# A mixture of experts on one core: a DRAIN one unit sooner, first products on ones, and four groups of transposes elsewhere in the head

## The chip, the cores and the metric

The kernel runs on one core of a Trainium2 chip. The metric is the device time of the kernel in microseconds; the runs of the kernel before gave 457.3, 457.4 and 457.6, and the median, 457.4 us, is what a changed kernel is compared with.

## The reference, cut to what matters

4096 tokens of 256 values go through a gate, which chooses two of eight experts for each. An expert is three layers (256 to 512, 512 to 512, 512 to 256). The reference computes all experts for all tokens and weights them; the kernel computes only those chosen.

```python
var = jnp.mean(x * x, axis=-1, keepdims=True)
xn = rms_w * (x * jax.lax.rsqrt(var + EPS))
gate = xn @ wg_W + wg_b + (genre_embed @ gg_W + gg_b)
gate_w = jax.nn.softmax(gate, axis=-1)
topk_w, topk_i = jax.lax.top_k(gate_w, TOP_K)
cw = jnp.sum(jax.nn.one_hot(topk_i, E, dtype=x.dtype) * topk_w[..., None], axis=-2)
h1 = jax.nn.relu(jnp.einsum('bsh,ehm->bsem', x, W1) + b1)
h2 = jax.nn.relu(jnp.einsum('bsem,emn->bsen', h1, W2) + b2)
out_e = jnp.einsum('bsen,enh->bseh', h2, W3) + b3
return x + jnp.einsum('bseh,bse->bsh', out_e, cw)
```

Here x has 64 x 64 tokens, `genre_embed` is one row of 64 values for each group of 64 tokens, and all is float32.

## The kernel before, in words

The order of the instructions on each engine is written out by hand (`tc.manual_schedule`); the framework adds the waits.

**The head.** x lies in SBUF as 32 columns of 128 tokens, loaded in eight groups of four (`load_x`; group j is `xin[j]`). The gate needs x with its 256 values on the partitions, so each group is transposed by TensorE in two halves c = 0, 1. `turn_pe(j, c, bank)` (line 247) writes four 128 x 128 transposes into one PSUM bank, `TB[bank]`, where `TB` is the banks 0, 1, 2, 5, 4. `turn_copy(n, eng, bank)` copies that bank to place n, on VectorE ("V", line 258) or ScalarE ("A", line 260). `turn` is one after the other. `gates` and `gates_2` multiply the copied places by the gate's weights (lines 265 and 278), `upright` and `upright_2` turn the result back (lines 291 and 284).

The first eight columns (part A, groups 0 and 1) are routed at once, so that the first expert units can start: `first_part` normalises, chooses two experts for each token (`choose`, VectorE), counts ranks on TensorE (`ranks`, lines 399 and 400), finds each token's place in its expert's list (`pick`), builds one-hot tables (line 535) and multiplies them out to the list of tokens (line 539). With that list GpSimd gathers the first unit's rows (line 844). While part A is in work, the other groups are transposed in between. `second_part` goes on with part B, of which `some(n)` sums squares of n columns on VectorE; `transpose_x(0)` turns the rows gathered for unit 0, and `layer1(0)` follows (line 1015). `third_part` stands between `layer1(0)` and `layer2(0)` (line 1025).

Ahead of all this, `busy(n)` (line 301) issues n transposes of the 128 x 128 identity into a bank that nobody reads yet. The identity is made by GpSimd; `ones` is a 128 x 128 tile that VectorE fills first of all (line 152).

**The units.** Eight units of 128 tokens, one for each expert, come first, then units of four, two or one tiles of 128 places. Line 1124 is the products of layers 1 and 2 in the larger units, lines 1246 and 1214 those of layer 3. The routing of part B (`rest`) runs on VectorE beside the first eight units; its last tables are multiplied in line 604. For each tile, `give` forms weighted rows on VectorE (line 1262) and GpSimd adds them to the output by an indirect DMA (line 1263). A write waits for writes of the unit before to land, since a token's row is read and written back.

**The tail.** The number and sizes of the last units depend on the data; `tc.Switch` chooses one of several programs for them. `steps` runs unit u's layers 1 and 2 with unit u - 1's layer 3 and writes. In the unit after the last (u = last) only the last unit's layer 3 and its writes remain. GpSimd gets one DRAIN in the tail (line 1556); the program's end (line 1638) has others on every engine, and SyncE's waits for the landing of all DMAs.

```python
            if u == last - 1:
                nc.gpsimd.drain()
```

Of the kernel before, what the change touches and what calls it, by code (L numbers as in the profile page):

```python
# [52 lines left out]
def kernel(  # L53
# [17 lines left out]
    nc = tc.nc  # L71
    V = nc.vector
    P = 128
# [12 lines left out]
    GA = NA // TPB  # L86
# [30 lines left out]
    PB = [psum.tile([P, 512], F32, tag=f"pb{k}", name=f"pb{k}") for k in range(8)]  # L117
# [6 lines left out]
    def ring(pool, shape, tag, bufs, b, dt=F32):  # L124

        if tag not in rings:
            rings[tag] = [buf(pool, shape, f"{tag}_{k}", dt) for k in range(bufs)]
        return rings[tag][b % bufs]
# [17 lines left out]
    ident = const.tile([P, P], F32, name="ident")  # L146
# [4 lines left out]
    ones = const.tile([P, P], F32, name="ones")  # L151
# [50 lines left out]
    def load_x(j, n=1):  # L202
        k = j % (NG - GA)
        nc.sync.dma_start(
            big[:, k : k + n], xr[:, j * TPB : (j + n) * TPB, :].rearrange("p (j k) h -> p j k h", j=n)
        )
# [26 lines left out]
    def squares(i, eng):  # L233
        xi = xin[i // TPB][:, i % TPB, :]
        if eng == "A":
            nc.scalar.activation(sqs[eng], xi, AF.Square, accum_out=ss[:, i : i + 1])
        else:
            V.tensor_tensor_reduce(sqs[eng], xi, xi, 1.0, 0.0, ALU.mult, ALU.add, ss[:, i : i + 1])

    def turn(j, c, n, eng, bank):  # L240

        turn_pe(j, c, bank)
        turn_copy(n, eng, bank)

    def turn_pe(j, c, bank):
        for k in range(TPB):
            nc.tensor.transpose(TB[bank][:, ts(k, P)], xin[j][:, k, ts(c, P)], ident)  # L247

    def turned(n):

        if n < 4:
            return hid[1][:, n]
        return bigf[:, 2 * TPB * H + (n - 4) * TPB * P :][:, 0 : TPB * P]

    def turn_copy(n, eng, bank):
        tp, xTc = TB[bank], turned(n)
        if eng == "V":
            V.tensor_copy(xTc, tp)
        else:
            nc.scalar.copy(xTc, tp)  # L260

    def gates(c, bufs):

        for q, n in enumerate(bufs):
            nc.tensor.matmul(
                PB[3][32 * q : 32 * q + 32, :],
                lhsT=wg_sb[:, c, :],
                rhs=turned(n),
                start=c == 0,
                stop=c == HC - 1,  # L270
            )

    def gates_2(bufs, bank):

        for q, ns in enumerate(bufs):
            for c, n in enumerate(ns):
                r = 32 * (2 * c + q)
                nc.tensor.matmul(bank[r : r + 32, :], lhsT=wg_sb[:, c, :], rhs=turned(n), start=True, stop=True)  # L278
# [19 lines left out]
    def busy(n):  # L298

        for _ in range(n):  # L300
            nc.tensor.transpose(PB[3][:, 0:P], ident, ident)

    class Part:

# [146 lines left out]
    def some(n):  # L451
        for _ in range(n):
            squares(left.pop(0), "V")

    def first_part():


        rw2 = gTs[0:HC, 0:P]
        load_x(0)
        nc.scalar.dma_start(wg_in, wg_W.rearrange("(c p) e -> p c e", p=P))  # L460
        load_x(1)
        nc.scalar.dma_start(rw2, rms_w.rearrange("(c p) -> c p", c=HC))
        load_x(2, 2)
        nc.scalar.dma_start(gg_sb[0:G, :], gg_W)
        load_x(4, 2)
        nc.scalar.sqrt(warm, ones[:, 0:E])
        V.memset(wg_sb, 0.0)
        V.memset(condT[G : G + 2, :, :], 1.0)
        V.memset(cw8B, 0.0)
        for k in range(3):  # L470
            V.memset(ring(run, [P, H], "xg", 3, k), 0.0)
        V.memset(cgR, 0.0)
        nc.gpsimd.dma_start(cwdA.rearrange("(p i) e -> p i e", p=P)[:, NA:NI, :], cw8B[:, NA:NI, :])
        busy(7)
        rwp, cps, gps = PB[7][:, P : P + HC], PB[7][0:G, 2 * P : 2 * P + B], PB[7][:, 3 * P : 3 * P + E]
        nc.tensor.transpose(rwp, rw2, ident[:HC, :HC])
        V.tensor_copy(rwT, rwp)
        for c in range(HC):
            V.tensor_scalar(wg_sb[:, c, 0:E], wg_in[:, c, :], rwT[:, c : c + 1], None, ALU.mult)
        for i in (2, 3):  # L480
            squares(i, "A")
        turn(0, 0, 0, "V", 0)
        turn(0, 1, 1, "A", 1)
        squares(0, "V")
        turn(1, 0, 2, "V", 2)
        squares(TPB + 2, "A")
        turn(1, 1, 3, "A", 3)
        squares(TPB + 3, "A")
        nc.tensor.transpose(cps, cond_sb, ident[:B, :B])
        for i in (1, TPB, TPB + 1):  # L490
            squares(i, "V")
        V.tensor_copy(condT[0:G], cps.unsqueeze(2).to_broadcast([G, B, REP]))
        for j in range(NG - GA, NG):
            load_x(j)
        nc.sync.dma_start(vecs[0 : E * MC, :], b1.rearrange("e (c p) -> (e c) p", p=P))
        nc.sync.dma_start(vecs[E * MC : 2 * E * MC, :], b2.rearrange("e (c p) -> (e c) p", p=P))
        load_weights(0, (0, 1))
        gates_2(((0, 1), (2, 3)), PB[3])
        nc.scalar.copy(gTs, PB[3])
        pA.norm(True)  # L500
        turn(GA, 0, 0, "A", 0)
        nc.tensor.matmul(gps, lhsT=condT.rearrange("g b r -> g (b r)"), rhs=gg_sb, start=True, stop=True)
        V.tensor_copy(ggate, gps)
        row_numbers(0)
        chosen = pA.choose(upright_2(PB[4]))
        for q in (1, 2, 3):
            turn(GA + q, 0, q, "A", q)
        turn_pe(GA, 1, 0)
        next(chosen)
        turn_pe(GA + 1, 1, 4)  # L510
        for _ in chosen:
            pass
        pA.ranks()
        V.tensor_tensor(
            mvA.rearrange("p (k i) e -> p k i e", k=TOPK),
            pA.ohe.rearrange("p k e i -> p k i e"),
            toka.unsqueeze(1).unsqueeze(3).to_broadcast([P, TOPK, NA, E]),
            ALU.mult,
        )
        row_numbers(1)  # L520
        pA.exps()
        gates(0, range(4))
        turn_pe(GA + 2, 1, 1)
        turn_copy(0, "A", 0)
        turn_copy(1, "A", 4)
        turn_copy(2, "A", 1)
        V.scalar_tensor_tensor(
            pA.slot, pA.inc[:, 1:].rearrange("p (e i) -> p e i", e=E), -1.0, pA.along(pA.adj), ALU.add, ALU.add
        )
        pA.pick(lo16A.rearrange("p (k i) -> p k i", k=TOPK))  # L530
        tabA = PB[7][:, 0:E]
        GH = GC // 4
        for g0 in range(0, GC, GH):
            hs = slice(g0, g0 + GH)
            V.tensor_tensor(
                ohA[:, :, hs], iotx[:, :, hs], lo16A[:, hs].unsqueeze(1).to_broadcast([P, P, GH]), ALU.is_equal
            )
            for g in range(g0, g0 + GH):
                nc.tensor.matmul(tabA, lhsT=ohA[:, :, g], rhs=mvA[:, g, :], start=(g == 0), stop=(g == GC - 1))
        pA.totals()  # L540
        turn(GA + 3, 1, 3, "A", 2)

        V.tensor_scalar(sa[:, 0:E], tabA, 0.0, float(NT), ALU.is_equal, ALU.mult)
        V.scalar_tensor_tensor(idxA, tabA, float(OFFA), sa[:, 0:E], ALU.add, ALU.add)
        V.tensor_copy(totA1, pA.tot)
# [19 lines left out]
    def second_part():  # L565

        j0 = GA + 4
        vps = PB[6][:, 384 : 384 + 2 * E * MC]
        pA.weights()
        some(1)  # L570
        nc.tensor.transpose(vps, vecs, ident[: 2 * E * MC, : 2 * E * MC])
        V.tensor_copy(vT.rearrange("p l e c -> p (l e c)"), vps)
        some(1)
        turn(j0, 0, 4, "A", 3)
        some(2)
        turn(j0 + 1, 0, 6, "A", 0)
        gates(1, range(4))
        some(2)
        transpose_x(0)
        nc.scalar.copy(gTs, PB[3])  # L580
        turn(j0, 1, 5, "V", 3)
        some(4)

    def third_part():

        turn(GA + 5, 1, 7, "V", 3)
        some(len(left))
        raw = upright()
        nc.scalar.copy(graw[:, NA : NA + 4 * TPB, :].rearrange("p (q k) e -> p q k e", q=4), raw)
        gates_2(((4, 5), (6, 7)), PB[7])  # L590
        nc.scalar.copy(gTs, PB[7])
# [955 lines left out]
    def steps(u0, u1, last):  # L1547
        for u in range(u0, u1):
            if u < last and paired(u):
                step_fast(u, last)  # L1550
            else:
                step(u, last)
                if u < last:
                    layer2(u)
            if u == last - 1:
                nc.gpsimd.drain()

    CUT = E + NQT - 2
# [44 lines left out]
    for k in tc.Switch(arm, len(ARMS), hint="tail"):  # L1603
# [5 lines left out]
        last = E + len(plan)  # L1609
# [33 lines left out]
```

## Time and profile before

| what | us |
|---|---|
| runs, median (lowest to highest) | 457.4 (457.3 to 457.6) |
| the profiled execution's own time | 457.79 |
| its span | 456.0 |
| busy: TensorE's products | 443.9 |
| busy: VectorE | 364.9 |
| busy: GpSimd | 270.8 |
| busy: ScalarE | 240.2 |
| first transpose of the identity | starts at 2.62 |
| first gather (unit 0) | issued at 19.66 |
| layer 1 of unit 0 | starts at 23.57 |
| the DRAIN of line 1556 | 8.925 long, from 439.0 |
| last write | issued at 450.64 |

Times within the profile count from the start of its span. The profiled execution's own time holds 1.8 us more than the span, and lies 0.4 us above the median of the runs, which were taken without a profile. "Busy" counts overlapping instructions of an engine once. A matmul's end in the profile is modelled and later than the start of the next one, so a series is read by its starts.

### The profile page before, as it was taken

How to read it: one execution, taken by the hardware profiler on the slowest of the kernel's cores; microseconds unless marked ns; L12 is line 12 of the kernel's file. 1: busy time of each engine (PE TensorE's matmuls, PEld its weight loads, DVE VectorE, ACT ScalarE, POOL GpSimd, SP SyncE). 2: the span in 40 equal slices, each digit the busy share in tenths (PEclk: the TensorE clock that was granted, in tenths of full speed). 3: DMA queues.
4: the chain of work that ended last, by engine and by line, in shares of the span. 5: the costliest groups of instructions: out<-in, count | busy, mean ns of one | idle time of the engine just before them, and what ended most of it. 6: DMA issues, size and time to landing. Idle time of an engine off the chain costs nothing.

```text
span 456.0 us, 9190 instructions
## 1 busy us (share of the span) xinstructions
PE 443.9 (97%) x2942; PEld 410.0 (90%) x2942; DVE 364.9 (80%) x961; ACT 240.2 (53%) x559; POOL 270.8 (59%) x231
## 2 busy tenths in 40 slices
PE   7899999999999999999999999999999999999993
PEld 5689999968989898989999999999999889999992
DVE  5887897269797979798988988887877887988861
ACT  4746553435646373828365656464464355565551
POOL 4255532867787868677675656578646645664222
PEclk9999999999999999999999999999999999999998
DMA  8699999793766858374655555666656664675322
GB/s 294 251 308 376 378 366 385 283 271 79 188 160 133 180 108 193 76 166 108 131 125 125 117 123 116 130 180 137 144 149 115 156 162 93 163 177 143 70 24 27
DMA packets 75631, 78.76 MB, mean 173 GB/s; under 512 B 34927, under 2 KB 64082, under 8 KB 75188
## 3 DMA queue, kind: packets, MB, share of 16 engines
q1 hardware_dynamic: 48976, 43.29, 30.0%
q0 software_dynamic: 14960, 17.47, 22.6%
q10 hardware_dynamic: 11636, 17.32, 11.9%
q8 instruction: 25, 0.41, 0.4%
q14 instruction: 34, 0.28, 0.2%
HBM read 62.60 MB, written 20.12 MB: 181 GB/s over the span
## 4 chain that ended last, share of the span: by engine, by line
PE 90%; issue 3%; DMA 2%; ACT 1%; POOLq 1%; DVE 0%; POOL 0%; ACTq 0%
PE pb L1124 52%; PE pb L1246 12%; PE pb L1214 11%; PE pb L1025 6%; PE pb L1015 5%; PE pb L247 1%; DMA out_dram<-ys,idxR 1%; PE pb L604 1%; DMA gTs<-in_L_cond_rms_w_dram 1%; PE pb L911 1%; DMA xg<-in_x_dram,idxA 1%; PE pb L278 1%; POOLq L1638 1%; POOL out_dram L1263 0%; PE pb L284 0%
## 5 line engine op out<-in xcount | busy, mean ns | idle before, releaser
L1263 POOL DMA_INDIRECT out_dram<-ys,idxR x59 | 96.7, 1639 | 94.7 <-DVE ys L1262 41.6
L1124 PE MATMUL pb<-hid,big 128*128 128x256 f32 (+7 forms) x456 | 83.4, 326 | 0.0
L1145 ACT ACTIVATE hid<-hid,bb 128x256 f32<-128x256 f32 (+13 forms) x148 | 70.4, 524 | 16.6 <-DVE hid L1142 9.9
L844 POOL DMA_INDIRECT cg<-cwdR,idxR x59 | 67.6, 1145 | 18.0 <-issue 17.4
L1124 PEld LDWEIGHTS pb<-hid,big 128*128 128x128 f32 x456 | 71.4, 191 | 5.1 <-issue 1.0
L1246 PE MATMUL pb<-w3r,hid 128*128 128x256 f32 (+3 forms) x280 | 66.2, 380 | 0.0
L1133 ACT COPY q1s<-pb 128x256 f32<-128x256 f32 (+7 forms) x54 | 25.4, 470 | 59.5 <-PE pb L1124 59.0
L1133 ACT COPY big<-pb 128x512 f32<-128x512 f32 (+7 forms) x57 | 27.1, 476 | 55.3 <-PE pb L1124 55.3
L1246 PEld LDWEIGHTS pb<-w3r,hid 128*128 128x128 f32 (+3 forms) x280 | 49.5, 185 | 6.9
L1124 PE MATMUL pb<-mixB,big 128*128 128x256 f32 (+7 forms) x304 | 55.4, 325 | 0.0
L1124 PE MATMUL pb<-hotA,big 128*128 128x256 f32 (+7 forms) x304 | 52.5, 326 | 0.0
L1124 PEld LDWEIGHTS pb<-mixB,big 128*128 128x128 f32 x304 | 47.9, 191 | 2.6
L1124 PEld LDWEIGHTS pb<-hotA,big 128*128 128x128 f32 x304 | 47.3, 191 | 2.8
L844 POOL DMA_INDIRECT xgE<-in_x_dram,idxR x31 | 34.2, 1102 | 17.0 <-issue 15.2
L1124 PE MATMUL pb<-mixX,iotx 128*128 128x128 f32 (+7 forms) x216 | 43.1, 322 | 0.0
L1124 PEld LDWEIGHTS pb<-mixX,iotx 128*128 128x128 f32 x216 | 34.9, 191 | 2.0
L844 POOL DMA_INDIRECT big<-in_x_dram,idxR x28 | 30.8, 1099 | 8.5 <-issue 7.3
L1145 ACT ACTIVATE hid<-pb,bb 128x128 f32<-128x128 f32 (+7 forms) x74 | 26.7, 411 | 14.3 <-PE pb L1124 12.7
L1025 PEld LDWEIGHTS pb<-hid,w2a 128*128 128x128 f32 x256 | 29.8, 192 | 1.1 <-issue 0.8
L1025 PE MATMUL pb<-hid,w2a 128*128 128x128 f32 x256 | 30.5, 276 | 0.0
L899 DVE STREAM_TRANSPOSE xT<-gTs 128x256 f32<-128x256 f32 x55 | 29.0, 632 | 0.0
L1124 PE MATMUL pb<-xT,w1r 128*128 128x128 f32 (+7 forms) x144 | 28.8, 322 | 0.0
(331 smaller groups left out, 814.2 us busy)
## 6 DMA issues: line engine op xcount, KB each, us to landing
w3r<-in_L_cond_W_dram ACTq DMA_DIRECT2D x17, 512.0 KB, 5.1
w2a<-in_L_cond_W_dram SPq DMA_DIRECT2D x8, 1024.0 KB, 13.2
w1r<-in_L_cond_W_dram ACTq DMA_DIRECT2D x16, 512.0 KB, 3.5
w1r<-in_L_cond_W_dram SPq DMA_DIRECT2D x11, 512.0 KB, 12.6
w3r<-in_L_cond_W_dram SPq DMA_DIRECT2D x10, 512.0 KB, 12.0
gTs<-scr SPq DMA_DIRECT2D x7, 512.0 KB, 4.4
out_dram<-in_x_dram SPq DMA_DIRECT2D x4, 768.0 KB, 10.7
big<-in_x_dram SPq DMA_DIRECT2D x4, 512.0 KB, 4.4
```

Of the source, the lines that this page charges most:

```text
L247: nc.tensor.transpose(TB[bank][:, ts(k, P)], xin[j][:, k, ts(c, P)], ident)
L278: nc.tensor.matmul(bank[r : r + 32, :], lhsT=wg_sb[:, c, :], rhs=turned(n), start=True, stop=True)
L844: return nc.gpsimd.indirect_dma_start(out=dst, out_offset=None, in_=src, in_offset=bass.IndirectOffsetOnAxis(ap=index(b), axis=0), bounds_ ...
L899: V.transpose(xT[:, :, s0 + k, :].rearrange("p c (b k) -> p k c b", b=SQ), shs[:, s0 + k].rearrange("p k (a c) -> p k c a", a=SQ),)
L1015: nc.tensor.matmul(ph, lhsT=w1[:, c, ts(m, P)], rhs=cols[:, c, :], start=(c == 0), stop=(c == HC - 1))
L1025: nc.tensor.matmul(ph, lhsT=w2[:, m, ts(n, P)], rhs=hid[0][:, m, 0:BT], start=(m == 0), stop=(m == MC - 1))
L1124: nc.tensor.matmul(bank[:, ts(n, self.w)], lhsT=w[:, c, ts(n, P)], rhs=x[:, c], start=new and n == 0 and c == 0, stop=n == HB - 1 and c == ...
L1133: nc.scalar.copy(self.q[(1, 6, 5).index(k)], self.tall(self.X if k == 5 else self.U))
L1145: nc.scalar.activation(out, src, AF.Relu, bias=ww[self.u][1][:, self.l, n : n + 1])
L1214: nc.tensor.matmul(bank[:, ts(j, H // 2)], lhsT=a[:, c, ts(j, P)], rhs=b[:, c], start=new and j == 0 and c == 0, stop=j == 1 and c == HB - ...
L1246: nc.tensor.matmul(sums(u, k)[0 : cols.stop - cols.start], lhsT=hid[1][:, n, cols], rhs=w3[:, n, :], start=(i == 0), stop=(i == MC - 1))
L1263: add = nc.gpsimd.indirect_dma_start(out=orows, out_offset=bass.IndirectOffsetOnAxis(ap=index(b)[0:n], axis=0), in_=y[0:n], in_offset=None ...
```

## The change

One DRAIN, the operands and number of the first products, and the places of five calls change; no instruction is moved between engines and no DMA is added or taken away.

- `busy` issues float32 products of `ones` with itself in place of transposes of the identity, and it is called for eight instead of seven.
- In `first_part`, the group (GA + 2, half 1, bank 1) is transposed ahead of `ranks` instead of behind `gates`; the group (GA + 3, half 1, bank 2) takes its old place, and only its copy stays where both were.
- In `second_part`, the group (j0, half 1) is transposed ahead of `transpose_x(0)`, into bank 2 instead of bank 3; the group (j0 + 1, half 1, bank 3), with j0 + 1 = GA + 5, takes its old place, from `third_part`. Their copies stay where they were.
- In `steps`, the DRAIN is issued at the end of unit last - 2 instead of last - 1.

```diff
     def busy(n):
 
         for _ in range(n):
-            nc.tensor.transpose(PB[3][:, 0:P], ident, ident)
+            nc.tensor.matmul(PB[3][:, 0:P], lhsT=ones, rhs=ones, start=True, stop=True)
...
-        busy(7)
+        busy(8)
...
         turn_pe(GA + 1, 1, 4)
         for _ in chosen:
             pass
+        turn_pe(GA + 2, 1, 1)
         pA.ranks()
...
         gates(0, range(4))
-        turn_pe(GA + 2, 1, 1)
+        turn_pe(GA + 3, 1, 2)
         turn_copy(0, "A", 0)
         turn_copy(1, "A", 4)
         turn_copy(2, "A", 1)
...
         pA.totals()
-        turn(GA + 3, 1, 3, "A", 2)
+        turn_copy(3, "A", 2)
...
         gates(1, range(4))
+        turn_pe(j0, 1, 2)
         some(2)
         transpose_x(0)
         nc.scalar.copy(gTs, PB[3])
-        turn(j0, 1, 5, "V", 3)
+        turn_pe(j0 + 1, 1, 3)
+        turn_copy(5, "V", 2)
         some(4)
 
     def third_part():
 
-        turn(GA + 5, 1, 7, "V", 3)
+        turn_copy(7, "V", 3)
         some(len(left))
...
-            if u == last - 1:
+            if u == last - 2:
                 nc.gpsimd.drain()
```

## The prediction

> **What bounds the kernel now.** The page first: busy shares, then the shares of the chain that ended last.
>
> ```profile
> PE 443.9 (97%) x2942; PEld 410.0 (90%) x2942; DVE 364.9 (80%) x961; ACT 240.2 (53%) x559; POOL 270.8 (59%) x231
> ...
> PE 90%; issue 3%; DMA 2%; ACT 1%; POOLq 1%; DVE 0%; POOL 0%; ACTq 0%
> ```
>
> TensorE carries 90% of the chain; the list of TensorE's waits names nobody between 28 and 449 us. So whatever is taken out ahead of 28 us moves everything behind it, and only head and tail have other owners. The timeline of TensorE in the head:
>
> ```profile
> 2.62 1.76 PE L301 MATMUL pb<-ident 128*128 128x128 f32 x7 [2.62 <-POOL ident masks.py:199]
> ...
> 5.05 3.68 PE L247 MATMUL pb<-ident,big 128*128 128x128 f32 x16
> ...
> 12.13 2.49 PE L247 MATMUL pb<-ident,big 128*128 128x128 f32 x20
> 15.29 0.39 PE L399 MATMUL pb<-incA,tri 128*128 128x8 f32 x2 [0.67 <-DVE d2A L394]
> ```
>
> The same transposes go at 0.213 us each from 5.05 and at 0.109 us each from 12.13: the clock has doubled between (the trace's grant of the full clock begins at 9.40). TensorE started at 2.62, waiting for GpSimd's identity, and stood still from 4.38 to 4.86. At 15.29 the rank products wait for VectorE. In the chain in order of time, around unit 0's first layer:
>
> ```profile
> 23.57 2.05 PE pb L1015 x16
> 25.62 0.44 PE pb L247 x4
> 26.06 0.44 PE pb L291 x4
> 26.49 1.39 PE pb L278 x8
> 27.89 1.98 PE pb L1025 x16
> ```
>
> The four transposes of line 247 at 25.62 stand between the two layers. Who waits for whom there, from the timeline of all engines:
>
> ```profile
> 12.65 1.73 PEld L247 LDWEIGHTS pb<-ident,big 128*128 128x128 f32 x16 [0.15 <-DMA big<-in_x_dram]
> ...
> 23.64 0.69 DVE L258 COPY big<-pb 128x512 f32<-128x512 f32 x1 [0.70 <-PE pb L247]
> ...
> 26.09 0.69 DVE L258 COPY big<-pb 128x512 f32<-128x512 f32 x1
> ...
> 26.84 0.14 PEld L278 LDWEIGHTS pb<-big,wg_sb 128*32 128x32 f32 x2 [0.27 <-DVE big L258]
> ```
>
> VectorE idles 0.70 us for a group of transposes at 23.64, and so comes late with its copy at 26.09, for which the last gate product (26.84) waits. The tail, in the timeline, then by line, then the DMA queue's own waits:
>
> ```profile
> 437.42 0.47 DVE L1262 SCALAR_TENSOR_TENSOR ys<-pb,cw,bc 128x256 f32<-128x256 f32 x1
> 438.17 1.55 POOL L1263 DMA_INDIRECT out_dram<-ys,idxR  x1 [9.16 <-DVE ys L1262]
> ...
> 446.89 0.48 DVE L1262 SCALAR_TENSOR_TENSOR ys<-pb,cw,bc 128x256 f32<-128x256 f32 x1 [1.49 <-PE pb L1246]
> ...
> 448.78 1.55 POOL L1263 DMA_INDIRECT out_dram<-ys,idxR  x1 [7.20 <-issue]
> 450.64 1.55 POOL L1263 DMA_INDIRECT out_dram<-ys,idxR  x1 [0.30 <-issue]
> ```
>
> ```profile
> L1556 POOLq DRAIN  x1: 8925/8925/8925, 439.0 to 439.0; - x1
> ...
> L1638 POOLq DRAIN  x3: 46/120/5037, 449.6 to 455.7; - x3
> ```
>
> ```profile
> SPq L1638 <- DMA out_dram<-ys,idxR: 10.6, 2, 8.7
> ```
>
> A write normally starts 0.28 us after its rows are ready (437.89 to 438.17). The first of the last unit is ready at 447.37 and starts at 448.78, because the DRAIN of line 1556 holds GpSimd until 439.0 + 8.9 = 447.9. The program ends on the landing of the very last write: by the trace's semaphore records 454.51, 3.87 after its start; SyncE ends its waits at 455.14 and the span ends 0.82 later. The profiled execution took 457.79 us with a span of 456.0; the median of the runs is 457.4, 0.39 less, so I take differences from the span and apply them to the median.
>
> **Part 1, the DRAIN.** It is moved past two writes only (those at 438.17 and 440.03); no gather or SyncE transfer stands between the places. In its new place it follows the write at 427.27, which occupies GpSimd until 429.01. Today's DRAIN ends 6.33 us after GpSimd's last write before it (447.91 - 441.58); 429.01 + 6.33 = 435.3, and GpSimd is next needed at 437.89: hidden with 2.5 us to spare, of which a write's own 0.5 us of issue after a DRAIN (448.06 to 448.56) takes a fifth. Were the cover gone, each us over would delay the write at 438.17, behind which GpSimd stands idle from 441.6 to 447.6: some 6 us more until it counts. The first of the last writes then starts at 447.37 + 0.28 = 447.65 instead of 448.78, the second after 1.55 + 0.31 at 449.51 instead of 450.64 (its rows are ready at 449.10): **-1.13 us**. Unknown is the final DRAIN, which now follows four writes since the last one instead of two. Today it ends 2.43 us after the last write's GpSimd time (449.58 + 5.04 = 454.62 against 452.19), 0.11 after the landing. Bounds: 2.43, and the 6.33 that a DRAIN over the whole program took. I take a value near 2.43, by the row with the nearest count: I read most of the 6.33 as the price of the many transfers before it (GpSimd has 231 instructions in all), and four are near two.
>
> **Part 2, the first products.** Eight float32 products, each shown as two records (as L399 is), make 16 at 0.213 = 3.4 us. They wait for the memset of `ones` (ends at 1.08) instead of the identity, so they run from 1.1 to about 4.6 or 4.8. The next step waits for its DMA until 4.86 anyway: cost 0, and whatever they overrun 4.86 by if the pace is worse. TensorE is then busy without a hole from 1.1 on, instead of from 4.86. Before, 4.5 us of unbroken work preceded the full clock, and a stretch of the same length from 1.1 ends at 5.6. About 12 of the 16 transposes then save 0.104 each, 1.2 us; ScalarE's copies between them let through about 1.0. But TensorE works in order, and the rows of x that it turns next land only at 12.61 (the wait at 12.65). From there come 16 transposes as before, and four more by part 3, last start 14.35 + 4 x 0.109 = 14.79, so the rank products stand at 14.89 instead of 15.29. From them to the gather's issue at 19.66 the chain is VectorE's and TensorE's and moves whole: **-0.40 us**. Ends: 0 (no earlier clock) and -0.6 (the transposes move for free). I take -0.40, the row at 12.65 setting it.
>
> The Trainium skill, "TensorE: Matmul & The Clock Gate", Part 4, says that transposes do not count as activity for the clock as products do, and Part 1 that a whole window of some 3.4 us must be busy. Our row speaks against the first: nearly everything before 9.40 was transposes and the clock rose. By the rule the new products would hardly fill one window alone and part 2 would be worth 0; the sum would be 455.6 instead of 455.2.
>
> **Part 3, the four groups of transposes.** Each is 4 x 0.109 = 0.44 us. The first goes ahead of the rank products, into the 0.67 us of waiting at 15.29: 0 by itself. The second takes the first one's old place: 0. The third goes between the gate products (20.85 to 21.9) and the transposes that wait for the gather (0.69 us idle before 22.60): 0. The fourth takes the third's old place (22.95): 0. The place at 25.62 becomes empty: TensorE saves 0.44. VectorE finds the third group done and copies at 22.94 instead of 23.64; its next copy ends at 26.08 instead of 26.78, so the last gate product starts at 26.14 instead of 26.84, where TensorE alone would allow 25.98. The later of the two counts: **-0.70 us**. New waits: the first group on ScalarE's copy out of its bank (done by 13.4), the third product of unit 0's first layer on VectorE's copy out of bank 2 (done by 23.7, needed at 24.5): 0. Next late are weights: by the semaphore records, unit 3's first-layer weights land at 46.79 and are read at 47.84, and a third-layer load lands at 63.92, read at 64.72. That stream starts with the first gather, so it moves by part 2's 0.40 too; against the 0.70 stand 1.05 and 0.80. Ends: -0.44 and -0.86 (VectorE early enough); I take -0.70.
>
> **Sum:** -1.13 - 0.40 - 0.70 = -2.23; 457.79 - 2.23 = 455.56 for a profiled execution, 455.2 for the median. Between no change and faster or slower, 0.2% (0.9 us) is what a measurement of this kernel can tell.
>
> **Rivals.**
> - *The final DRAIN pays back.* If it needs the full 6.33 after four writes, it ends at 451.06 + 6.33 = 457.39 instead of 454.62, and the span at 458.2: tail +2.3, head -1.10, **458.6, slower**. It decides from 2.95 us on (SyncE's waits, 455.14 - 1.13, less 451.06). At 1.21 us per write (2.43 / 2) it is 4.85 and the sum 457.1. For it: nothing shows why two writes cost 2.43; against: 2.43 ends just behind a landing.
> - *The clock rises no sooner* (at 9.40 again): **455.6**. For it: one hole of 0.48 us in 4.5 need not be what held the clock down; against: that hole goes, and the work begins 1.5 us sooner.
> - *The DRAIN gives nothing,* because GpSimd is held by something else before the last writes, and the change does not do there what it says: **456.3**. For it: 0.5 us of issue behind the DRAIN; against: the unit before started 0.28 after its rows.
> - *Weights or VectorE swallow the head's 0.70*: **455.9**. For it: 0.80 us of slack; against: the list of TensorE's waits is empty there.
>
> **How the numbers follow.** Forecast 0.53; clock 0.15; weights 0.08; DRAIN without gain 0.09; DRAIN paid back at 457.1, 0.06, at 458.6, 0.09. Range 454.6 to 456.5: from -0.6 and -0.86 in the head (-0.36 together) and a further 0.2 of scatter, up past the third rival. Outside lie the paid-back cases, 0.15. Faster by over 0.2%: 0.53 + 0.15 + 0.08 + 0.09 = 0.85 (below 456.5); within: 0.06; slower: 0.09.
>
> **What would show it.** Right: transposes at 0.11 from about 6 us; rank products near 14.9; no line 247 between L1015 and L291, L1025 near 26.7; a DRAIN that ends before 437; last writes 1.55 and 0.3 apart, 0.28 behind their rows; a final DRAIN that ends with the last landing. Wrong: transposes still at 0.21 at 8 us, a wait of TensorE on weights between 30 and 70 us, or a final DRAIN ending over 0.5 us behind SyncE's waits.

## The result and the profile after

The changed kernel ran at a median of 456.77 us (455.34 to 458.03, 20 runs) against 457.88 (457.06 to 459.43, 20 runs) for the kernel before: ratio 0.9974, interval 0.9963 to 0.9984. It is faster by about 0.26%, some 1.1 us, half of the 2.2 that were forecast, and 456.77 lies above the range's end of 456.5. Ratios here and below leave out runs more than 1.5% above the fastest of their kernel, which matters mainly under "Runs that decide little". The runs are of two kinds. Spans (first to last instruction; the time is 1.8 more) are 453.6 to 454.6 in five of the twenty, with a mean granted clock of .997 or .998, and 454.8 to 456.3 in the rest, with .992 to .996. The profiled execution, span 456.3, is the longest of all; its page:

```profile
PE 446.6 (98%) x2951; PEld 413.2 (91%) x2951; DVE 365.2 (80%) x961; ACT 240.2 (53%) x559; POOL 272.1 (60%) x231
...
PEclk9899999999999999999999999999999999999998
...
PE 83%; DMA 7%; issue 5%; POOL 2%; DVE 1%; POOLq 1%; SPq 0%; DVEq 0%
```

The row PEclk, the clock granted to TensorE in 40 slices, has an 8 in its second slice (11.4 to 22.8 us) where the kernel before had 9. TensorE is busy 2.7 us longer than before, and its share of the chain fell from 90% to 83%, DMA's rose from 2% to 7%. The timeline of TensorE in the head (start, duration, what, count, idle before):

```profile
1.13 3.78 PE L301 MATMUL pb<-ones 128*128 128x128 f32 x16 [1.13 <-DVE ones L152]
...
5.04 2.72 PE L247 MATMUL pb<-ident,big 128*128 128x128 f32 x16
...
10.25 1.08 PE L284 MATMUL pb<-both,gTs 128*128 128x64 f32 x8
11.17 0.61 PE L247 MATMUL pb<-ident,big 128*128 128x128 f32 x4
13.03 4.07 PE L247 MATMUL pb<-ident,big 128*128 128x128 f32 x20 [1.26 <-DMA big<-in_x_dram]
16.94 0.29 PE L399 MATMUL pb<-incA,tri 128*128 128x8 f32 x2
```

The first products start at 1.13 and the clock did rise sooner, at 6.62 instead of 9.40. But the twenty transposes at 13.03 take 4.07 us, 0.2 each: they run at half clock again. The trace's grants are full from 6.62 to 13.45, half from 13.45 to 16.86, full from there. So the rank products stand at 16.94, not at the forecast 14.9. They no longer wait for VectorE, which has done the last of what they wait for (d2A) by 14.32 and then itself waits 2.92 us for them:

```profile
14.18 0.14 DVE L394 TENSOR_TENSOR d2A<-cw8A,prA 128x8 f32<-128x8 f32 x1
...
17.54 0.22 DVE L528 SCALAR_TENSOR_TENSOR gateA<-incA,pb 128x64 f32<-128x64 f32 x1 [2.92 <-PE pb L400]
```

The same stretch by the clock's own windows (start to end; length; busy time and records of PE, PEld, DVE, ACT, POOL; granted clock; DMA share; GB/s):

```profile
6.62:10.03 3.41, 3.41 (x25) 2.04 (x23) 2.78 (x12) 2.38 (x8) 0.00 (x0) 1.00 1.07 336
10.03:13.45 3.42, 2.11 (x19) 1.81 (x18) 2.62 (x13) 2.19 (x5) 0.34 (x1) 1.00 0.94 355
13.45:16.86 3.41, 3.41 (x19) 3.41 (x17) 1.10 (x5) 2.69 (x4) 0.00 (x0) 0.50 1.03 400
```

TensorE stood still for 1.26 us in the second window, waiting for x, and exactly the window after it was granted half the clock. Around unit 0 the chain in order of time has lost line 247, as forecast:

```profile
25.15 2.05 PE pb L1018 x16
27.20 0.44 PE pb L291 x4
27.64 1.10 PE pb L278 x8
28.73 1.31 PE pb L1028 x10
```

From the gathered rows' first transposes to unit 0's second layer (L1028; L1025 before) it is 4.48 us instead of 5.22. Behind it, one wait of TensorE on weights has appeared, in the list of its waits (total, times, longest):

```profile
PE pb L1249 <- DMA w3r<-in_L_cond_W_dram: 0.2, 1, 0.2
```

The tail, GpSimd's timeline, then the lines of the two DRAINs:

```profile
428.74 1.74 POOL L1266 DMA_INDIRECT out_dram<-ys,idxR  x1 [0.31 <-DVE iotx L1079]
439.64 1.55 POOL L1266 DMA_INDIRECT out_dram<-ys,idxR  x1 [9.16 <-DVE ys L1265]
...
449.11 1.55 POOL L1266 DMA_INDIRECT out_dram<-ys,idxR  x1 [6.06 <-DVE ys L1265]
450.97 1.55 POOL L1266 DMA_INDIRECT out_dram<-ys,idxR  x1 [0.30 <-issue]
```

```profile
L1559 POOLq DRAIN  x1: 9079/9079/9079, 427.6 to 427.6; - x1
...
L1641 POOLq DRAIN  x3: 46/120/3990, 451.0 to 456.0; - x3
```

The moved DRAIN ends at 427.62 + 9.08 = 436.70, before the write at 439.64 needs GpSimd. The first of the last writes starts 0.28 behind its rows (448.83), the second 1.86 later, and the final DRAIN ends at 455.03, 0.21 behind the last landing (454.83).

### The profile page after: what moved, and what is told of

Same layout as the page of the kernel before. It is cut to its first block, busy times and chain, and to the rows that moved or that the text cites. A ratio compares the mean times of both kernels' runs of the same rounds, so it can differ in the third digit from the quotient of the medians.

```text
span 456.3 us, 9211 instructions
## 1 busy us (share of the span) xinstructions
PE 446.6 (98%) x2951; PEld 413.2 (91%) x2951; DVE 365.2 (80%) x961; ACT 240.2 (53%) x559; POOL 272.1 (60%) x231
## 4 chain that ended last, share of the span: by engine, by line
PE 83%; DMA 7%; issue 5%; POOL 2%; DVE 1%; POOLq 1%; SPq 0%; DVEq 0%
PE pb L1127 50%; PE pb L1217 11%; PE pb L1249 10%; PE pb L1028 5%; PE pb L1018 4%; DMA w3r<-in_L_cond_W_dram 3%; DMA big<-in_x_dram 2%; POOL out_dram L1266 1%; PE pb L247 1%; PE pb L607 1%; DMA out_dram<-ys,idxR 1%; DMA xg<-in_x_dram,idxA 1%; PE pb L914 1%; POOLq L1559 0%; POOL cg L847 0%
## 5 line engine op out<-in xcount | busy, mean ns | idle before, releaser
L1028 PEld LDWEIGHTS pb<-hid,w2a 128*128 128x128 f32 x256 | 29.8, 192 | 1.1 <-ACT graw L592 0.8
L1028 PE MATMUL pb<-hid,w2a 128*128 128x128 f32 x256 | 30.5, 276 | 0.0
```

The lines of the kernel that those rows point to most:

```text
L1028: nc.tensor.matmul(ph, lhsT=w2[:, m, ts(n, P)], rhs=hid[0][:, m, 0:BT], start=(m == 0), stop=(m == MC - 1))
```

## The experiments

The stages of one profiled execution of each kernel, in us; the runs follow below. "Ranks" is the first weight load of the rank products, "E" the first layer of the first larger unit; between the two last writes lie 1.86 us more.

| kernel | 0 to ranks | to the gather's issue | to the gathered rows on TensorE | to unit 0's layer 2 | to E | to the last unit's rows | to its first write | last write to the end | span |
|---|---|---|---|---|---|---|---|---|---|
| before | 15.29 | 4.37 | 2.94 | 5.22 | 63.30 | 356.25 | 1.41 | 5.32 | 455.96 |
| after | 16.79 | 4.40 | 2.99 | 4.48 | 63.88 | 356.29 | 0.28 | 5.33 | 456.30 |
| e1_drain | 15.42 | 4.38 | 2.94 | 5.22 | 63.30 | 356.26 | 0.28 | 5.26 | 454.92 |
| e2_groups | 15.30 | 4.38 | 2.96 | 4.52 | 63.33 | 356.27 | 1.43 | 5.33 | 455.38 |
| e3_products | 14.60 | 4.38 | 2.95 | 5.21 | 63.33 | 356.28 | 1.38 | 5.22 | 455.20 |
| e4_old_products | 15.19 | 4.39 | 2.99 | 4.48 | 64.30 | 356.27 | 0.28 | 5.22 | 454.98 |
| a3_again (= after) | 15.09 | 4.38 | 2.87 | 4.59 | 63.33 | 356.27 | 0.28 | 5.18 | 453.84 |
| e5b_filled | 14.88 | 4.39 | 2.97 | 4.49 | 63.32 | 356.28 | 0.28 | 5.23 | 453.70 |
| e9_no_groups | 14.57 | 4.39 | 2.92 | 5.22 | 63.32 | 356.26 | 0.27 | 5.24 | 454.05 |
| e7_no_drain | 14.78 | 4.38 | 3.98 | 4.47 | 63.33 | 356.29 | 0.27 | 8.73 | 458.09 |

### One part at a time

**e1_drain**: the kernel before with only the DRAIN moved.

```diff
-            if u == last - 1:
+            if u == last - 2:
                 nc.gpsimd.drain()
```

> The kernel before with the DRAIN alone moved. Theory (the DRAIN's gain is real and the head lost what was expected of it): the first last write starts 0.28 us behind its rows, the final DRAIN ends within 0.3 us of the last landing, and the median is 1.1 us lower (0.9 to 1.3), with the spread of the kernel before. Rival (the final DRAIN pays back): 0 to 0.5 us lower, the final DRAIN ending over 0.5 us behind SyncE's waits.

Measured: 456.30 (12 runs) against 457.53 beside it, ratio 0.9967 (0.9954 to 0.9979): 1.23 us. In the table only one stage changes by more than 0.13 us, 1.41 to 0.28: the forecast 1.13. The kernel before, too, has runs of two kinds: 9 of its 34 beside this one have a mean clock of .992 or .993 and spans of 456.5 to 457.4, the other 25 a clock of .995 and more and a median of 457.29. None of e1_drain's twelve is under .996, though its head is that of the kernel before; so part of the 1.23 is luck, and against the 25 it gains 1.0.

**e2_groups**: the kernel before with only the four groups moved (the five calls of the diff; `busy` and the DRAIN as before).

> The kernel before with the four groups of transposes alone moved. Theory: layer 2 of unit 0 starts 0.70 us sooner after the gather's landing (4.5 instead of 5.2 us from the first transposed gathered row to line 1025), and the median is 0.7 us lower (0.4 to 0.9). Rival (weights swallow it): the 0.7 is there at 28 us and gone by 70, TensorE waiting for a third-layer weight load near 65, and the median is 0 to 0.3 lower. Rival (the group ahead of the rank products delays them): rank products 0.2 us later or more, median 0.3 lower.

Measured: 457.75, ratio 0.9996 (0.9981 to 1.0011): no gain clear of the noise, between 0.9 us faster and 0.5 slower. Yet layer 2 comes after 4.52 us instead of 5.22, the forecast 0.70. Six of its twelve runs have a mean clock of .992 to .994 and spans of 455.9 to 457.2, the others .995 to .997 and 455.1 to 455.9. So half of the runs seem to lose the 0.70 again somewhere. Its timeline:

```profile
13.17 2.40 PE L247 MATMUL pb<-ident,big 128*128 128x128 f32 x20 [0.74 <-DMA big<-in_x_dram]
15.41 0.29 PE L399 MATMUL pb<-incA,tri 128*128 128x8 f32 x2
```

The rank products follow the twentieth transpose at once and wait for nobody. VectorE is done at 15.00 in this execution, their first weight load stands at 15.30: the group set ahead of them costs 0.3 of its 0.44 us.

**e3_products**: the kernel before with only the first products changed.

```diff
-            nc.tensor.transpose(PB[3][:, 0:P], ident, ident)
+            nc.tensor.matmul(PB[3][:, 0:P], lhsT=ones, rhs=ones, start=True, stop=True)
...
-        busy(7)
+        busy(8)
```

> The kernel before with the first products alone changed (eight products of ones instead of seven transposes). Theory (the clock, once raised early, falls back for one stretch of 3.4 us when TensorE runs ahead of x and stands still from about 11.8 to 13 us): runs of two kinds, most with a mean granted clock of .992 to .995 that take 0 to 0.8 us longer than before, some with .997 or more that take 0.4 to 0.8 us less; median from 0.4 lower to 0.5 higher, spread 2 us or more. Rival (it is the x rows that land later, the clock changes nothing): no clock below that of the kernel before, all runs 0 to 0.4 us longer. Rival (it is the moved group in front of the rank products): without it, as here, 0.4 to 0.8 us lower in all runs.

Measured: 456.94, ratio 0.9985 (0.9972 to 0.9998): 0.59 us. Eleven of twelve spans lie within 455.1 to 455.6, one at 456.6 with a clock of .992; the wide scatter that I expected did not come. Against the 25 runs without a low clock (457.29) the gain is 0.35, near the forecast 0.40. Rank products at 14.60.

**e4_old_products**: the changed kernel with the seven transposes of the identity back in `busy`.

> The changed kernel with the seven transposes of the identity back as first work. Theory (the first products are what spoils the sum): 1.13 + 0.74 = 1.9 us below the kernel before (1.5 to 2.1), and so 0.7 us below the changed kernel, with rank products at 15.3. Rival (weights or the moved groups spoil it): 1.1 us below, like the changed kernel, with a wait of 0.3 us on a weight load near 65 us.

Measured: 456.68, ratio 0.9976 (0.9960 to 0.9991), 0.85 us, where the changed kernel gained 1.1 in its own comparison and 1.3 in another (a3_again below). So the first products are not what spoils the sum, and the theory was wrong: taking them out of the change costs 0.3 to 0.5 us. Its profiled execution loses 1.00 us between layer 2 and E, the changed kernel's 0.58, the others at most 0.03.

### What makes the clock fall

**a3_again** is the changed kernel once more; **e5b_filled** gives TensorE work in its hole:

```diff
         for q in (1, 2, 3):
             turn(GA + q, 0, q, "A", q)
+            if q == 1:
+                busy(5)
```

> The changed kernel itself, once more, as the yardstick of this call. All theories: as in the first comparison, some 1.1 us below the kernel before, over a spread of 455.3 to 458.0 (wider than the 1.4 us of the kernel before). Theory of the stand-still: spans of two kinds, some 453.6 to 454.4 where the clock does not fall in the head, some 455.5 to 456.5 where it does.

> The changed kernel, with five more products of ones issued behind the transposes of the second group, so that TensorE has work where it stood still from 11.78 to 13.03 for the rows of x. Theory of the stand-still (the clock fell because of it): no fall of the clock in the head in any run, the rank products at 14.9 to 15.1, the upper part of the changed kernel's times goes, median 1.0 to 1.3 us below the changed kernel's. Rival (the fall is drawn by chance, whatever TensorE does there): the same spread and the same median as the changed kernel's, within 0.4 us. Second rival (what is won in the head is eaten by waiting for weights between 30 and 70 us): no fall, but the median within 0.4 us of the changed kernel's.

Measured, before beside them 457.67: a3_again 456.35 (10 runs), ratio 0.9971 (0.9957 to 0.9985). Four spans are 453.8 to 453.9 with clocks of .997 to .999, six are 454.5 to 455.7 with .992 to .994: two kinds indeed. e5b_filled 456.26 (6 runs, 455.50 to 456.65), ratio 0.9963 (0.9949 to 0.9976). The changed kernel's runs above 456.7 are gone, but the median is only 0.1 lower: my figure of 1.0 to 1.3 was missed, and the rivals' (within 0.4 us) came true. The profiled executions of both had no fall. First a3_again's timeline, then that of e5b_filled:

```profile
5.16 2.04 PE L247 MATMUL pb<-ident,big 128*128 128x128 f32 x16
...
12.95 2.40 PE L247 MATMUL pb<-ident,big 128*128 128x128 f32 x20 [1.74 <-DMA big<-in_x_dram]
15.19 0.29 PE L399 MATMUL pb<-incA,tri 128*128 128x8 f32 x2
```

```profile
11.13 1.28 PE L301 MATMUL pb<-ones 128*128 128x128 f32 x10
12.75 2.40 PE L247 MATMUL pb<-ident,big 128*128 128x128 f32 x20 [0.34 <-DMA big<-in_x_dram]
14.99 0.29 PE L399 MATMUL pb<-incA,tri 128*128 128x8 f32 x2
```

In a3_again TensorE stood still for 1.74 us, longer than in the first profile of the same kernel (1.26), and the clock stayed: idle time alone does not decide. There is a second place, which the run without a DRAIN showed. **e7_no_drain**: the changed kernel without the DRAIN inside the tail.

```diff
-            if u == last - 2:
-                nc.gpsimd.drain()
```

> The changed kernel without the DRAIN inside the tail; only the one at the program's end is left. Theory (a DRAIN's price goes with how many writes lie before it: 6.2 to 6.3 us behind GpSimd's last write after a whole program, 2.4 to 2.5 after two to four): the final DRAIN ends some 6.3 us behind GpSimd's last write instead of 2.5, so the span ends 3.4 us later (SyncE's waits now end 0.44 us behind the DRAIN), the median 3.0 to 3.8 us above the changed kernel's. Rival (the price is flat, some 2.5 us or the wait for the last landing, and the 6.2 us belongs to the place in the middle of the writes): the same time as the changed kernel within 0.4 us.

Measured: 459.70, ratio 1.0035 (1.0021 to 1.0049), 3.35 above a3_again; the theory held. The line of the final DRAIN:

```profile
L1639 POOLq DRAIN  x3: 46/120/7810, 449.4 to 457.8; - x3
```

It ends at 457.24, 6.33 behind GpSimd's last write (450.91), though SyncE saw the last landing by 453.7. So most of its length is not the wait for a landing: it ends 2.3 to 2.6 behind the last write wherever another DRAIN stands two or four writes back, and 6.1 to 6.4 where nearly the whole program lies behind it. Counted from the last landing, the twenty traces agree more closely. A DRAIN ends 0.12 behind it with two writes since the DRAIN before (before, e2, e3), 0.20 or 0.21 with four (the sixteen others that have one in the tail), 3.98 with all but the last four writes behind it, 4.06 with all but two, and 4.14 in e7_no_drain, with all. So the short ones end just behind the landing, and each write more adds some 0.04 us. In its head (windows as above, then the timeline):

```profile
16.38:19.80 3.42, 2.96 (x30) 2.58 (x29) 2.64 (x12) 2.57 (x7) 0.65 (x1) 1.00 0.69 251
19.80:23.21 3.41, 3.41 (x17) 1.42 (x16) 2.49 (x13) 1.17 (x2) 2.79 (x5) 0.50 0.28 79
```

```profile
17.14 1.33 PE L540 MATMUL pb<-mvA,hotA 128*128 128x8 f16 x16 [0.16 <-DVE hotA L536]
18.33 0.37 PE L405 MATMUL pb<-incA,ones 128*128 128x9 f32 x2
19.00 0.27 PE L572 MATMUL pb<-ident,vecs 64*128 64x64 f32 x1 [0.31 <-DVE totA L546]
```

Here the clock fell after a window in which TensorE was busy for 2.96 of 3.41 us. What fills it are the sixteen table products, which stream eight columns each. The fall costs 1.03 us between the gather's issue and the gathered rows (3.98 for 2.95); in the four heads below that fell at the same place, up to layer 2, 0.7 to 1.1.

So I counted, for every clock window in the heads of all twenty profiled executions (starts up to 25 us), the time in which TensorE streams columns: 0.109 us for 128 columns at full clock (the pace of line 247), a quarter of that for the f16 columns of the table products, and products that run side by side counted once. This is an estimate after the event, worked out from those traces:

| kernel, start of the window | streamed share | clock after it |
|---|---|---|
| e7_no_drain 16.38 | 0.30 | falls |
| after 10.03 | 0.36 | falls |
| highest of the eight windows that fell (e6_short_copy 17.44) | 0.37 | falls |
| lowest that stayed (a4_again 8.87) | 0.39 | stays |
| e3_products 14.71 | 0.41 | stays |
| e7_no_drain 9.56 | 0.42 | stays |
| a3_again 11.23 (hole of 1.72 us) | 0.48 | stays |

Of 112 windows at full clock, the eight that fell are the eight lowest. The quarter is an assumption that no run here tests: with f16 columns counted in full, the highest that fell comes to 0.395 and the lowest that stayed to 0.393, so the line is no sharper than that.

The windows that the count had not used agree. Behind the heads lie 2509 more at full clock, up to the end of TensorE's work. The clock fell after 25 of them (in the kernels of the last part of this section), all with a share of 0.37 or less; only two of the others are under 0.41 (0.372 and 0.388, both in the last microseconds). The same line shows on the way up: of 72 windows at half clock, counted at the full clock's pace, the clock stayed down after the 19 with up to 0.39 and rose after the 53 with 0.40 and more. TensorE's busy share has no such line: a window 91% busy fell (e6_short_copy 17.44), one 50% busy stayed (a3_again 11.23).

Transposes count like products in this, and the windows' grid has another phase in every run (its steps are 3.413 us: 443.73 / 130 in the kernel before). The Trainium skill, "TensorE: Matmul & The Clock Gate", Part 1, has such a free-running window of 3.4 us, which these grants show; its table lets the clock fall after an idle window, and in these heads it fell after windows that were 59 to 91% busy. Part 4's rule that transposes do not count finds no support: a3_again's window from 11.23 holds nothing but transposes, and the clock stayed.

With a limit of 0.38 the traces tell for how many phases of the grid a window falls. With the first pair of groups moved, a window that starts between 15.72 and 17.46 (a3_again; 15.94 to 17.68 in e2_groups) is too thin: half of all phases. With the pair in its old place it is 15.70 to 16.10 (e9_no_groups): one in nine. One group is 0.44 us, 0.13 of a window, and it used to stand in the hole behind the table products. The hole for x makes starts from 9.00 to 10.34 too thin in a3_again. Two steps of the grid on, these are 15.83 to 17.17: the same phases, so the hole adds hardly any, but a run that falls there loses 1.4 to 1.9 us ahead of the rank products (after, a5_again, e10b_late_groups) instead of about 1 us behind them. So e5b_filled takes away the dear fall and leaves the cheap one: three of its six runs have clocks of .992 to .994 and spans of 454.4 to 454.9.

For the runs without a profile only the mean clock is known. It is a rough mark, since it also holds a stretch at the program's end that varies with the phase. It was .994 or less in 29 of 60 runs with the first pair moved (after 11 of 20, e2 6 of 12, e4 3 of 12, a3 6 of 10, e5b 3 of 6) and in 13 of 78 without (before 12 of 48, e1 0 of 12, e3 1 of 12, e9 0 of 6). That goes roughly with half of the phases and with one in nine. It does not go with e3_products' own hole for x, which by the same count is too thin for starts from 8.94 to 10.24, two phases in five, where one run of twelve fell; that stays open. No kernel was made to test the figure of 0.38 alone.

**e9_no_groups**: e1's and e3's edits together, the groups where they were.

> The kernel before with two of the three parts, the DRAIN one unit sooner and the eight products of ones; the four groups of transposes stand where they were. By the sum of the two parts run alone (1.23 and 0.59): 1.8 us below the kernel before, and 0.6 us below the changed kernel, since without the moved groups TensorE reached the rank products at 14.60 and the clock did not fall. Rival (the groups are worth their 0.70 us, and the fall would come here as well): 0.4 to 0.7 us above the changed kernel.

Measured: 455.86 against 457.67, all six runs within 455.77 to 456.21, clocks .996 to .998; ratio 0.9953 (0.9940 to 0.9966). That is the sum of the two parts alone, no run of six with a low clock, and the lowest ratio of all, 0.5 us below the changed kernel on the same chip (their intervals overlap). Its timeline:

```profile
12.87 1.97 PE L247 MATMUL pb<-ident,big 128*128 128x128 f32 x16 [0.98 <-DMA big<-in_x_dram]
14.68 0.29 PE L399 MATMUL pb<-incA,tri 128*128 128x8 f32 x2
...
18.13 0.37 PE L405 MATMUL pb<-incA,ones 128*128 128x9 f32 x2
18.36 0.63 PE L247 MATMUL pb<-ident,big 128*128 128x128 f32 x4
18.92 0.27 PE L571 MATMUL pb<-ident,vecs 64*128 64x64 f32 x1
```

The group at 18.36 fills what is a hole from 18.70 to 19.00 in e7_no_drain, and the rank products follow sixteen transposes instead of twenty.

### Runs that decide little

All kernels of the three sets below, the one before included, took some 470 to 489 us (one run of the kernel before 1635), because TensorE stood still in mid-kernel (in a5_again once for 5.6 us) and its clock fell there; their totals scatter, and only their heads are read.

The first set: a2_again (the changed kernel), e5_filled (as e5b_filled), e6_short_copy (e5_filled with a shorter first copy of x to the output) and e8_late_reload (e5_filled, with the seventh group of x loaded behind the third).

```diff
-fills.append(nc.sync.dma_start(our[:, 0:NA, :], xr[:, 0:NA, :]))
+fills.append(nc.sync.dma_start(our[:, 0:1, :], xr[:, 0:1, :]))
```

```diff
-            load_x(j)
+            again = load_x(j)
+            if j == NG - GA:
+                tc.add_manual_dep(
+                    again.ins,
+                    third.ins.name,
+                    mybir.DependencyInfo(mybir.DependencyClass.Sync, mybir.DependencyReason.DATA),
...
+                )
```

> The changed kernel once more, beside the others of this call. Theory (the clock falls back in part of the runs): two kinds of runs again, span 453.6 to 454.6 without the fall and 454.8 to 456.3 with it; median 456.8, 0.8 to 1.1 below the kernel before. Rival (one slow profile, nothing more): one kind of run, within 0.6 us of each other.

> The changed kernel with five more products of ones (ten records, 1.1 us at the full clock) behind the transposes of group GA + 1, in the place where TensorE stood still from 11.8 to 13.0; nothing else changes and the products are never read. Theory (the stand-still lets the clock fall): no fall of the clock in the head in the profile, the rank products at 14.9 to 15.3, and nearly all runs like those without a fall: median 455.9 (455.4 to 456.3), 0.9 below the changed kernel. Rival (late x rows and weights are the loss): the same median as the changed kernel or 0 to 0.3 more, since the products can only be in the way.

> As the last one, but of the first copy of x to the output (the first eight columns, 1 MB read and 1 MB written amid the weight loads) only the first column is copied, so that 7 MB in 8 of it are left out and the output lacks x in these rows. Theory (the second loss is the stream of weights, which the earlier TensorE now meets): TensorE waits for no weight, line 1025 to the first unit of eight (91 us) takes 63.3 us as in the kernel before, and the median is 0.3 to 0.7 below the one with the whole copy. Rival (weights are only late by the chance of one profile): 0 to 0.1 below.

> As the filled one, but the seventh group's load of x waits for the landing of the third load (groups 2 and 3). Theory (the earlier copies let that load start before the others have landed, and it takes bandwidth from the rows that are turned next): the load starts at 8.9 or later, groups 4 and 5 land at 12.6 instead of 13.0, the rank products stand 0.3 to 0.4 sooner, and the median is 0.3 lower than the filled one's. Rival (they land late for another reason): 12.9 to 13.1 again, and the median 0 to 0.3 higher.

Measured: 474.27, 475.82, 476.10 and 475.11 against 478.0 for before; ratios 0.9933 (0.9894 to 0.9971), 0.9935 (0.9893 to 0.9978), 0.9947 (0.9903 to 0.9991), 0.9896 (0.9830 to 0.9963): not told apart. Rank products at 14.89, 14.93, 15.08 and 15.03: neither less traffic nor a later reload brought x sooner. In the three filled ones the clock fell in the table products' window (at 19.48, 20.85 and 20.57), not in the filled hole.

The second set: a4_again, e9b_no_groups, and **e10_late_groups** (only the second pair of groups is moved) with its filled twin e11_late_filled. The third: a5_again and e10b_late_groups. The edit of e10_late_groups against the changed kernel:

```diff
-        turn_pe(GA + 2, 1, 1)
         pA.ranks()
...
-        turn_pe(GA + 3, 1, 2)
+        turn_pe(GA + 2, 1, 1)
...
-        turn_copy(3, "A", 2)
+        turn(GA + 3, 1, 3, "A", 2)
```

> The changed kernel as the yardstick of this call: two kinds of runs again, spans near 453.8 with a clock of .997 and more, and 454.5 to 456.3 with .992 to .995; median 456.3 to 456.8.

> The DRAIN and the eight products of ones without the four moved groups, a second time: as the first time, all runs within 0.5 us, median 455.9, clock .996 to .998. If the narrowness was luck of six draws: some runs at 456.5 and above with a clock of .992 to .994.

> The changed kernel with only the second pair of groups moved (the one between the gate products and the gathered rows, and the one that left the place between the two layers of unit 0); the first pair stands where it stood. Theory (the first pair does the harm: the group ahead of the rank products costs them its 0.44 us, since the rows of x land late, and the pair leaves TensorE emptier while the list of tokens is made, where the clock fell): rank products at 14.6, unit 0's second layer 0.7 us earlier than without moved groups, span 453.4, nearly no run with a fall, median 455.2 to 455.4, which is 0.6 below the kernel without moved groups. Rival (any later place of work in the head moves the first half against the clock's windows, and the second pair does the harm as well): a wide spread, median 456.0 and above.

> The kernel with the second pair of groups only, and the five products of ones where TensorE stands still for the rows of x. Theory: the fill costs nothing and takes away what falls of the clock are left at that place: median 455.1 to 455.4, within 0.2 of the kernel without the fill, and no run over 456. Rival (the falls do not come from the stand-still): the same spread as without the fill.

> The changed kernel as the yardstick of this call: median some 1.1 to 1.3 us below the kernel before; the lower part of its runs 2 us below it, the upper part at or near it.

> The changed kernel with only the second pair of groups moved, once more. Theory (the first pair does the harm): rank products at 14.6, unit 0's second layer at 26.4, span 453.3 to 453.5; median 2.2 to 2.5 us below the kernel before and about 1 us below the changed kernel, all runs within some 0.6 us. Rival (the second pair does harm as well): a spread of 2 us and a median within 0.4 us of the changed kernel's.

Measured: 484.43, 484.27, 483.77 and 483.93 against 486.64 (ratios 1.0001, 0.9899 to 1.0102; 0.9928, 0.9821 to 1.0035; none for the third, of which a single run is left for it; 0.9957, 0.9863 to 1.0052), then 483.35 and 482.29 against 483.59 (0.9975, 0.9885 to 1.0064; 0.9971, 0.9880 to 1.0062). No order can be read from these totals, so whether e10_late_groups beats e9_no_groups stays open. Its head is as the theory has it, in e10_late_groups' timeline:

```profile
14.68 0.29 PE L399 MATMUL pb<-incA,tri 128*128 128x8 f32 x2
...
22.87 2.05 PE L1017 MATMUL pb<-xT,w1r 128*128 128x128 f32 x16
24.75 0.60 PE L291 MATMUL pb<-ident,gTs 128*128 128x128 f32 x4
```

Unit 0's second layer starts at 26.43 there, 27.13 in e9b_no_groups, 27.82 in the kernel before. But e10b_late_groups, with the same code, had the fall after the window of its hole for x (9.42 to 12.83, streamed share 0.32) and its rank products at 16.07: the wait for x remains as a trap of the earlier clock. The heads of the changed kernel in these sets show all three cases: no fall (a2_again), one at the tables (a4_again, at 19.11) and one at the hole for x (a5_again, at 12.56, rank products at 16.47). Those of e9b_no_groups, e10_late_groups and e11_late_filled had none.

## Why the prediction was wrong

- **Part 1, the DRAIN: right**, in size (1.41 to 0.28, the forecast 1.13) and in what it rests on. The moved one ends 6.22 behind its write, hidden; the final one 2.51 behind the last write, not 6.33. The rival in which it pays back is out: it reckoned with 1.21 us per write, and behind the landing the traces show 0.04. e7_no_drain shows what the DRAIN is worth: 3.35 us.
- **Part 2, the first products: right as a term, wrong in a premise.** Alone they gave 0.59 us in the median, within the changed kernel 0.3 to 0.5; the forecast was 0.40. Without a fall the rank products stood where the forecast had them (14.88 in e5b_filled, 14.89 in a2_again, 15.09 in a3_again; forecast 14.89). But "from there come 16 transposes as before, and four more" took it for granted that a clock once risen stays. In the first profile, the slowest of the twenty runs, it fell, the twenty transposes took 4.07 us instead of 2.40, and the term became +1.50 instead of -0.40. I had weighed only when the clock would rise; that it could fall again stood in no rival. Nor is "4.5 us of unbroken work" what it takes to rise: with the old first products the clock rose at 7.53 to 9.42 in the four profiled executions, with the new ones at 4.41 to 7.20, by the phase of the grid.
- **Part 3, the groups: the step that failed for the median.** The term of -0.70 at layer 2 was there (5.22 before, 4.47 to 4.59 in the six with the groups moved). The zeros for the first pair were wrong. "Into the 0.67 us of waiting at 15.29: 0 by itself" holds only where the clock rises as late as 9.40: with the early one VectorE is done by 14.3 (after), TensorE does not wait for it, and the group costs its 0.44 (14.57 without it in e9_no_groups, 15.09 with it in a3_again). And taking the other group out of the hole behind the table products ("takes the first one's old place: 0") thins a clock window, which by the count half of the phases pay for with about 1 us. So the groups alone brought no gain that can be told (e2_groups), and with the other two parts the median is 0.5 us higher with them than without (456.35 and 455.86), where it was to be 0.70 lower. This 1.2 us is as much as the sum fell short by (1.1 for 2.23), but the medians' intervals overlap: the falls are shown, their price in the median is in part argued.
- **The weights**: between layer 2 and E the first profile lost 0.58 and e4_old_products 1.00, the other eight of the table at most 0.03. In the first profile the third-layer load that the text had named landed at 66.02 and was waited for, in e4_old_products at 64.83, read at 64.93. Why in these two executions is open, and so is how often it happens in runs without a profile.
- **The sum** was -2.23. The profiled executions without a fall have -2.12 (a3_again) and, filled, -2.26 (e5b_filled). So the sum describes one kind of run. Four in ten, or five in twenty, were of that kind, and the median belongs to the other. It was chance that the three runs and the profile on which I built (457.3 to 457.6, clock .997) show only the better kind of the kernel before; over twenty runs its median is 457.88. That the falls make the difference is shown in the profiled executions; for the other runs it is read from their mean clock.

## What to carry to other kernels

Work that fills a hole of TensorE can be worth its time twice: before moving it, ask what the granted clock does to everything behind the hole. A median of runs that come in two kinds is not forecast by adding up one trace; look for what the kinds differ in (here the clock column), in the kernel before as well, and price both. And a zero that rests on a wait is to be looked at again when another part of the same change removes that wait.

## What the hardware showed

- TensorE's clock changes on a grid of 3.413 us whose phase differs from run to run. In the twenty profiled executions it fell after windows whose streamed share was 0.37 or less and came back after one of 0.40 or more, by the count above (an estimate). In the heads TensorE was busy for 2.0 to 3.1 us in the windows that fell, and the clock stayed through a hole of 1.72 us with a share of 0.48. There each fall lasted one window; in mid-kernel, where TensorE streamed little at half clock too, up to three (10.24 us in a4_again).
- GpSimd's DRAIN ends 6.1 to 6.4 us behind the last write when no other stands before it, 2.3 to 2.6 when one stands two or four writes back. In every trace it ends behind the last landing: 0.12 us with two writes since the DRAIN before, 0.2 with four, 4.14 with the whole program's.
